# Four edits around a 16-state scan in a fused two-layer kernel: constants loaded in the first stage, the first unit in three banks, an output projection by channels, and a gate placed behind the next scan

## The chip, the core and the metric

The kernel runs on one core of one Trainium2 chip. The metric is the device time of one execution in microseconds. Everything is float32. Engines are named as in the profile: PE (TensorE), DVE (VectorE), ACT (ScalarE), POOL (GpSimd), and SP, whose queue issues the DMAs.

## The reference

An image batch `x` of 4 x 128 channels x 64 x 64 goes through two layers.

Layer 0 normalises `x` by groups, computes a score per 4 x 4 patch with two depthwise convolutions, sorts the 256 patches of each image by score, and runs a selective scan over the 4096 pixels in that order. Its inner width is 256, its state 16. With `xz = x1n @ in_proj_w.T` split into `xm` and `z`:

```
xc = silu(conv1d(xm) + b);  dbc = xc @ x_proj_w.T
dt = softplus(dt_low @ dt_proj_w.T + dt_proj_b)
h  = exp(dt * A) * h + dt * B * xc          # 256 x 16 states, step by step
y  = (h . C + D * xc) * silu(z);  out_m = y @ out_proj_w.T
```

`out_m` is put back into the pixel order and added to `x`. Layer 1 runs a scan with 256 states over the 4096 tokens of each image, adds its output, and then adds a spectral convolution with 16 filters. This second layer takes most of the time and none of its arithmetic is touched here.

## The kernel before

The program is one function, `conv_attn_hybrid` (L1504), with three stages.

**First stage**, `layer0_front` (L24): the four images one after the other, `tokens` (normalising, turning into patches) of the next image beside `ordered` (convolutions, scores, sorting) of this one, plus the matrices of the spectral part. The order of its instructions is written by a planner with costs, not by hand. At its end each image's sorted tokens, `xn`, are evicted from PSUM by eight ACT instructions (L293) and stored to `xnt` in DRAM (L295). The permutation goes to `permd`.

**Scan stage**, `layer0_scan` (L338), whose order is written out by hand (`manual_schedule`). The work is cut into 32 units, 8 per image, of 512 tokens. A unit has 16 steps: two halves of 256 tokens by 8 pairs of states. All 512 steps run in one loop (L632). In step `j` the loop issues: the loads of B and C for `j+5` (`fetch`, SP), the scan's input for `j+3` (`spread`, POOL), the scan's factors for `j+1` (`lift`, four Exp on ACT), the scan itself, its product with C and a copy of the last state (`scan`, DVE), and the sum over states of step `j-1` (`add_up`, two PE matmuls into the bank `y`, and at the end of a half two more with `diag`, which holds D). When a half is complete, `gated` (L581) multiplies `y` by the silu of z on DVE; `y` has one PSUM bank, so the next half's first `add_up` waits for it.

Beside the steps, `beside` (L607) moves three kinds of work forward through one more PSUM bank, `mm`: `project` (the next unit's projections: convolution as four matmuls with premultiplied taps, z, Silu, B/C/dt, Softplus), `output` (out_proj of the finished unit) and `put_back` (permutation back, and the sum with the image). Each is a generator; a step lets at most one of them use `mm` ("mm"), and its eviction ("post") follows a step later.

Before the loop the stage loads its constants through SP (L364 to L380), among them all four permutations (`perm_t`), prepares some on DVE and ACT, and runs `project` of the first unit from start to end, one bank, one step after another (L602). Before that, `layer1_weights` (L750) puts the loads of layer 1's weights on SP. `output` computes, for each of the 16 pixels of a patch, 32 patches x 128 channels, with the gated values as weights of the matmul (L462): 32 rows of the array's output. `put_back` loads half an image into `xs`, which has one buffer, at the moment it needs it (L476).

**Layer 1**, `layer1` (L906): 8192 steps of a 256-state scan (L1314), in an order written by hand.

## Time and profile before

| | us |
|---|---|
| median of three runs | 21104.62 (21103.96 to 21105.43) |
| profiled execution, its own time | 21106.96 |
| its span, first to last instruction | 21105.0 |
| first stage, to the last store of `xnt` (L295) | 0 to 548 |
| scans of the 16-state stage (L554), first to last start | 614.78 to 2674.68 |
| scans of layer 1 (L1314), first to last start | 2710.48 to 20998.3 |
| DVE busy | 20433.2 (97%) |
| POOL busy | 19751.2 (94%) |
| PE busy | 17551.7 (83%) |
| ACT busy | 15761.0 (75%) |

A group of the profile names line, engine, operation, what is written and what is read, shape and count; behind the bar stand busy time and the mean duration of one in ns, then the idle time of the engine just before these instructions and what ended most of it. In the order of time, a row has start, duration, engine, line, operation, count and, in brackets, idle time and its releaser. A matmul of float32 leaves two records.

### The profile page before, as it was taken

The page shows a single profiled execution, that of the slowest core. Times are in us where ns is not written, and L with a number is a line of the kernel's source. Part 1 is how long each engine was busy: PE and PEld are TensorE (multiplying, and loading weights), DVE is VectorE, ACT ScalarE, POOL GpSimd, SP SyncE. Part 2 cuts the span into 40 slices and gives each one's busy share as a digit, 9 for nine tenths or more (in the row PEclk, how much of TensorE's full clock was granted, in tenths as well). Part 3 has the DMA queues.
Part 4 walks back from the last instruction along what each step waited for, and adds up shares of the span by engine and source line. Part 5 has one row for each costly group of instructions (what it writes and reads, how often), then busy time and mean ns, then how long its engine had stood idle before and what let it go on. Part 6 is the DMA issues. An engine that isn't in the chain of part 4 may idle for free.

```text
span 21105.0 us, 282109 instructions
## 1 busy us (share of the span) xinstructions
PE 17551.7 (83%) x99112; PEld 7740.7 (37%) x99112; DVE 20433.2 (97%) x11824; ACT 15761.0 (75%) x28195; POOL 19751.2 (94%) x3541
## 2 busy tenths in 40 slices
PE   7788844655858888877868999599999999999998
PEld 4344421322323333343323344243434434434434
DVE  7799999999999999999999999999999999999997
ACT  3667667777777777777777777787887777788876
POOL 2666699999999999999999999999999999999997
PEclk8999966776979999998979999699999999999999
DMA  1555554555656666665656777577777777777775
GB/s 69 133 142 143 145 162 156 183 174 172 219 174 224 222 226 224 222 211 196 210 186 223 231 239 238 173 238 236 238 235 232 235 234 235 237 235 233 232 231 182
DMA packets 2194842, 4287.94 MB, mean 203 GB/s; under 512 B 768744, under 2 KB 1288208, under 8 KB 1928080
## 3 DMA queue, kind: packets, MB, share of 16 engines
q1 hardware_dynamic: 2193424, 4269.90, 63.3%
q8 instruction: 784, 12.85, 0.2%
q14 instruction: 634, 5.19, 0.1%
HBM read 3645.09 MB, written 623.91 MB: 202 GB/s over the span
## 4 chain that ended last, share of the span: by engine, by line
DVE 51%; issue 15%; PE 12%; POOL 5%; ACT 4%; DMA 1%; DVEq 0%; SPq 0%; POOLq 0%; ACTq 0%
DVE ring L1314 49%; PE conv L1257 6%; POOL ring L1298 4%; PE yp L1344 3%; ACT da L1310 2%; PE fin L1199 1%; ACT conved L1269 1%; DMA strip<-in_phi 0%; ACT t L804 0%; PE mm L883 0%; PE mm L877 0%; PE mm L868 0%; PE mm L1039 0%; PE conv L1111 0%; ACT ye L1351 0%
## 5 line engine op out<-in xcount | busy, mean ns | idle before, releaser
L1298 POOL TENSOR_TENSOR ring<-u,dlb 128x4088 f32<-128x4088 f32 x2048 | 18075.4, 8889 | 67.4 <-DMA dlb<-delta 37.7
L1314 DVE TENSOR_TENSOR_SCAN ring<-da,ring 128x1024 f32<-128x1024 f32 x8192 | 17927.7, 2263 | 180.4 <-ACT da L1310 149.6
L1310 ACT ACTIVATE da<-dlb,at 128x511 f32<-128x511 f32 x16384 | 11321.1, 691 | 4049.2 <-DVE ring L1314 3763.3
L1257 PE MATMUL conv<-strip,tok 128*128 128x512 f32 (+3 forms) x20224 | 8569.6, 551 | 46.0 <-DMA strip<-in_phi 45.0
L1344 PE MATMUL yp<-ring,c 128*32 128x256 f32 x65536 | 4917.1, 428 | 2493.9 <-DVE ring L1314 1283.8
L1257 PEld LDWEIGHTS conv<-strip,tok 128*128 128x128 f32 x20224 | 3606.1, 191 | 4105.8 <-issue 3722.3
L1344 PEld LDWEIGHTS yp<-ring,c 128*32 128x32 f32 x65536 | 2007.5, 119 | 6188.5 <-issue 3468.9
L532 POOL TENSOR_TENSOR v<-dx,bcb 128x1024 f32<-128x1024 f32 x512 | 1208.8, 2361 | 633.0 <-DVE states L554 629.4
L1199 PE MATMUL fin<-conved,pq 128*128 128x512 f32 (+1 forms) x3840 | 1750.5, 549 | 9.2 <-ACT sum L1220 4.8
L546 ACT ACTIVATE f<-dt,an 128x255 f32<-128x255 f32 x2048 | 974.7, 476 | 493.0 <-DVE states L554 442.3
L554 DVE TENSOR_TENSOR_SCAN states<-f,v 128x1024 f32<-128x1024 f32 x512 | 1176.0, 2297 | 106.3 <-ACT f L546 54.7
L1351 ACT COPY ye<-yp 128x512 f32<-128x512 f32 x2048 | 1185.9, 579 | 24.5 <-PE yp L1344 23.4
L570 PE MATMUL y<-p,ident 128*128 128x512 f32 x2048 | 1008.6, 618 | 173.5 <-DVE p L558 170.0
L1269 ACT COPY conved<-conv 128x512 f32<-128x512 f32 x1664 | 963.0, 579 | 146.3 <-PE conv L1257 143.2
L1199 PEld LDWEIGHTS fin<-conved,pq 128*128 128x128 f32 x3840 | 644.5, 192 | 385.8 <-issue 278.0
L558 DVE TENSOR_TENSOR p<-states,bcb 128x1024 f32<-128x1024 f32 x512 | 627.0, 1225 | 38.3 <-DVE states L554 0.5
L570 PEld LDWEIGHTS y<-p,ident 128*128 128x128 f32 x2048 | 363.6, 193 | 709.1 <-issue 336.8
L1304 ACT COPY ring<-vf 128x8 f32<-128x8 f32 x2048 | 386.8, 189 | 4.1 <-DMA omd<-om 4.1
L462 PE MATMUL mm<-ow,yg 128*32 128x128 f32 x2048 | 250.8, 276 | 39.2 <-ACT om L466 37.7
L462 PEld LDWEIGHTS mm<-ow,yg 128*32 128x32 f32 x2048 | 219.3, 133 | 136.4 <-ACT om L466 60.8
L1357 ACT COPY last<-ring 128x8 f32<-128x8 f32 x1792 | 267.2, 198 | 0.0
L407 PE MATMUL mm<-xin,taps 128*128 128x512 f32 x512 | 236.4, 605 | 23.2 <-DVE f L384 20.0
(242 smaller groups left out, 5484.3 us busy)
## 6 DMA issues: line engine op xcount, KB each, us to landing
dlb<-delta SPq DMA_DIRECT2D x2048, 1024.0 KB, 5.3
strip<-in_phi SPq DMA_DIRECT2D x1536, 448.0 KB, 5.0
yd<-ye SPq DMA_DIRECT2D x2048, 256.0 KB, 4.6
bcb<-bcd SPq DMA_DIRECT2D x1024, 256.0 KB, 4.3
strip<-in_phi SPq DMA_DIRECT2D x1024, 256.0 KB, 4.9
pq<-pqd SPq DMA_DIRECT2D x1408, 64.0 KB, 4.4
yt<-yd SPq DMA_DIRECT2D x4096, 4.0 KB, 4.4
pq<-pqd SPq DMA_DIRECT2D x256, 128.0 KB, 4.2
```

The source lines that it names most:

```text
L532: nc.gpsimd.tensor_tensor(v, ready[n][2][:, :, bass.ts(i, SUB)].unsqueeze(1).broadcast_to((128, 2, 2, SUB)), bc[:, 0].unsqueeze(2).broadca ...
L546: nc.scalar.activation(factors[j % 2][:, a, k, 1:], ready[n][1][:, k, SUB * i + 1 : SUB * i + SUB], AF.Exp, scale=an[:, k, 2 * g + a : 2 * ...
L554: nc.vector.tensor_tensor_scan(states.rearrange(flat), factors[j % 2].rearrange(flat), v.rearrange(flat), 0.0, ALU.mult, ALU.add)
L570: nc.tensor.matmul(t.rearrange("p k t -> p (k t)"), ident, p[:, a].rearrange("p k t -> p (k t)"), start=g == 0 and a == 0, stop=False, ski ...
L1199: nc.tensor.matmul(fin[:, bass.ds(c0, w)], pq[:, n, :], u[:, bass.ds(c0, w)], start=begin and n == 0, stop=end and not partly, skip_group_ ...
L1257: nc.tensor.matmul(ps[:, skip:], tok[:, 1 - r if side else r, j, :], strip[:, bass.ds(c0 - lo, TS - skip)], start=which == 0 and j == js[0 ...
L1269: nc.scalar.copy(u[:, cols], ps[:, cols])
L1298: nc.gpsimd.tensor_tensor(ring[:, q % NQ, :, :, 1:], ready[0][:, :, 1:].unsqueeze(1).broadcast_to((128, VD, 2, TS - 1)), dl[:, :, 1:].unsq ...
L1310: nc.scalar.activation(da[:, h, 1:], dl[:, d % VD, 1:], AF.Exp, scale=at[:, h, d : d + 1])
L1314: nc.vector.tensor_tensor_scan(v, da.rearrange("p h t -> p (h t)"), v, 0.0, ALU.mult, ALU.add)
L1344: nc.tensor.matmul(yp[i // 2][bass.ts(p, 32), i % 2], c[:, h, t], moving(h, 128 * i + 32 * p, 32), start=h == 0, stop=h == 1,)
L1351: nc.scalar.copy(ye, yp[j].rearrange("p i d t -> p i t d"))
```

## The change

- `scan_constants` allocates the scan stage's constants before the first stage. `bring` issues their loads in the first stage while its second image is worked on, `prepare` computes with them during the third. `perm_t` is no longer loaded whole.
- In the first stage, four of the last image's eight evictions of `xn` go to DVE.
- The first unit is projected by `opening`, which uses the banks `mm` and `y` and the two of `states`, splits the Silu, takes its last product on DVE and issues the factors of steps 0 and 1. The second unit's projection is begun (its `xin` load) before it.
- `output` first multiplies all 512 tokens by `out_proj_w` with channels as rows, copies that (`yo`), and then turns it with matmuls against the identity: five turns at the bank `mm` and not four.
- `put_back`'s two halves of the image and its permutation are loaded when the output of an image's last unit begins (`place_of`), into two buffers.
- `gated` is issued between the scan and the product of the next step but one, and in that step `beside` goes ahead of `add_up`.
- Layer 1's weights are loaded in step 10 of the scan stage and not before it. The tile `om` gets a pool of its own, and the pools are in another order.

```diff
@@ layer0_front
-            nc.scalar.activation(ranked[:, o : o + 2, :], ps, AF.Identity, bias=nb, scale=ng)
+            if b == NB - 1 and o % 4:
+                nc.vector.tensor_scalar(ranked[:, o : o + 2, :], ps, ng, nb, ALU.mult, ALU.add)
+            else:
+                nc.scalar.activation(ranked[:, o : o + 2, :], ps, AF.Identity, bias=nb, scale=ng)
...
         first.go(1)
+        if b == 1:
+            bring()
+        if b == 2:
+            prepare()
@@ new
+def scan_constants(nc, cp, w, ident):
...
+    def bring():
+        for t, src in to:
+            nc.sync.dma_start(t, src)
+
+    def prepare():
+        for i in range(4):
+            nc.vector.tensor_tensor(taps[:, i, :], taps[:, i, :], win[:, 0:256], ALU.mult)
+        for k in range(2):
+            nc.vector.tensor_scalar(diag[:, k, :], ident, dd[:, k : k + 1], None, ALU.mult)
+        nc.scalar.activation(an, an, AF.Exp)
+        nc.vector.tensor_scalar(an, an, -1.0, None, ALU.mult)
@@ layer0_scan
-    cp = ctx.enter_context(tc.tile_pool(name="b_c", bufs=1))
+    rare = ctx.enter_context(tc.tile_pool(name="b_om", bufs=1))
+    sm = ctx.enter_context(tc.tile_pool(name="b_sm", bufs=1))
     big = ctx.enter_context(tc.tile_pool(name="b_big", bufs=2))
-    sm = ctx.enter_context(tc.tile_pool(name="b_sm", bufs=1))
...
+    def opening(into, xin):
+        xz, dt, dx, af, bcd = into
+        z = states.rearrange("p n k t -> p n (k t)")
+        other = lambda: ps_.tile([128, 512], F32, tag="y", name="other")
+        banks = middle(), other()
+        for k in range(2):
+            for i in range(4):
+                nc.tensor.matmul(
+                    banks[k], taps[:, i, bass.ts(k, 128)], xin[:, bass.ds(i, PJ)], start=i == 0, stop=i == 3
+                )
+            nc.scalar.activation(xz[:, k, :], banks[k], AF.Identity, bias=cb[:, k : k + 1])
+        for k in range(2):
+            nc.tensor.matmul(z[:, k], win[:, bass.ts(2 + k, 128)], xin[:, 3:], start=True, stop=True)
+        nc.vector.tensor_copy(xz[:, 2:4, :], z)
+        nc.scalar.activation(xz[:, 0:2, :], xz[:, 0:2, :], AF.Silu)
+        ps = middle()
+        for k in range(2):
+            nc.tensor.matmul(ps[:96], xw[:, k, :], xz[:, k, :], start=k == 0, stop=k == 1)
+        nc.scalar.activation(xz[:, 2:4, :], xz[:, 2:4, :], AF.Silu)
...
+        banks = other(), middle()
+        for k in range(2):
+            nc.tensor.matmul(banks[k], dw[:, bass.ts(k, 128)], bc[0:8, :], start=True, stop=True)
+            nc.scalar.activation(dt[:, k, :], banks[k], AF.Identity, bias=db[:, k : k + 1])
+        nc.scalar.activation(dt, dt, AF.Softplus)
+        nc.vector.tensor_tensor(dx, dt, xz[:, 0:2, :], ALU.mult)
+        lift(0)
+        lift(1)
+        factors_of_carry(dt, af)
@@ output
-        yr = yg.rearrange("p k (r o) -> p k o r", o=16)
         rows = bass.ts(unit % 4, 32)
+        if unit == L // PJ - 1 and b < NB - 1:
+            for h in range(2):
+                place_of(b, h)
+        yield "mm"
+        ps = middle()
+        for k in range(2):
+            nc.tensor.matmul(ps, ow[:, k, :], yg[:, k, :], start=k == 0, stop=k == 1)
+        yield "post"
+        yo = sm.tile([128, PJ], F32, tag="yo", name="yo")
+        nc.scalar.copy(yo, ps)
+        yr = yo.rearrange("c (r o) -> c o r", o=16)
         for o in range(0, 16, 4):
             yield "mm"
             ps = middle()
             for i in range(4):
-                for k in range(2):
-                    nc.tensor.matmul(
-                        ps[rows, bass.ts(i, 128)], yr[:, k, o + i, :], ow[:, k, :], start=k == 0, stop=k == 1
-                    )
+                nc.tensor.matmul(ps[rows, bass.ts(i, 128)], yr[:, o + i, :], ident, start=True, stop=True)
@@ put_back
+    def place_of(b, h):
+        xs = sm.tile([128, 8, 4, 64], F32, tag="xs", name="xs", bufs=2)
+        nc.sync.dma_start(xs.rearrange("c py oy x -> c (py oy x)"), x[b][:, bass.ts(h, L // 2)])
+        perm = sm.tile([128, 2, 128], F32, tag="perm", name="perm", bufs=2)
+        nc.sync.dma_start(perm, permd[:, b, :, bass.ts(h, 128)])
+        places.append((xs, perm))
@@ scan
         nc.vector.tensor_tensor_scan(
             states.rearrange(flat), factors[j % 2].rearrange(flat), v.rearrange(flat), 0.0, ALU.mult, ALU.add
         )
+        if gate:
+            gated(j - 2)
@@ the loop over steps
-    for _ in project(*units[0], ready[0]):
-        pass
-    fronts, extra, rear, holder = [], [], None, None
-    ahead = [1]
+    xin = big.tile([128, 3 + PJ], F32, tag="xin", name="xin")
+    nc.sync.dma_start(xin, xnt[0][:, 0 : 3 + PJ])
+    ready[1] = tiles()
+    fronts, extra, rear, holder = [Work(project(*units[1], ready[1]))], [], None, None
+    opening(ready[0], xin)
+    ahead = [2]
...
-        if 0 <= j + 1 < steps:
+        if 1 < j + 1 < steps:
             lift(j + 1)
...
-        if j >= 2 and (j - 2) % pairs == pairs - 1:
-            gated(j - 2)
-        prods[j] = scan(j, vs.pop(j), bcs.pop(j))
+        if j == 10:
+            load_weights()
+        gate = j >= 2 and (j - 2) % pairs == pairs - 1
+        prods[j] = scan(j, vs.pop(j), bcs.pop(j), gate)
+        if gate:
+            beside(j)
         if j:
             add_up(j - 1, prods.pop(j - 1))
-        beside(j)
+        if not gate:
+            beside(j)
@@ conv_attn_hybrid
+    early = ExitStack()
+    constants = early.enter_context(tc.tile_pool(name="b_c", bufs=1, side="right"))
+    consts, bring, prepare = scan_constants(nc, constants, w, ident)
+    layer0_front(tc, ident, half, w, x, xnt, permd, pqd, mud, bring, prepare)
...
+    early.close()
     layer1(tc, ident, weights, work, psum, second, w["phi"], pqd, mud, x, omd, permd, first, x2, x3, out)
```

More of the change, by code (lines that the diff above doesn't have):

```diff
@@ L23, in layer0_front @@
 @with_exitstack
-def layer0_front(ctx: ExitStack, tc, ident, half, w, x, xnt, permd, pqd, mud):
+def layer0_front(ctx: ExitStack, tc, ident, half, w, x, xnt, permd, pqd, mud, bring, prepare):
     nc = tc.nc
@@ L334, with later, halves, layer0_scan @@
 PJ = 512
+def scan_constants(nc, cp, w, ident):
+    to = []
+    def later(name, shape, src):
+        t = cp.tile(shape, F32, name=name)
+        to.append((t, src))
+        return t
+    def halves(name, src):
+        return later(name, [128, 2], src.rearrange("(k p) -> p k", p=128))
+    win = later("win", [128, 512], w["in_proj_w"])
+    taps = later("taps", [128, 4, 256], w["conv1d_w"].partition_broadcast(128))
+    cb = halves("cb", w["conv1d_b"])
+    xw = later("xw", [128, 2, 96], w["x_proj_w"].rearrange("(k p) m -> p k m", p=128))
+    dw = later("dw", [8, 256], w["dt_proj_w"])
+    db = halves("db", w["dt_proj_b"])
+    dd = halves("dd", w["D"])
+    an = later("an", [128, 2, NS], w["A_log"].rearrange("(k p) n -> p k n", p=128))
+    ow = later("ow", [128, 2, 128], w["out_proj_w"].rearrange("(k p) c -> p k c", p=128))
+    diag = cp.tile([128, 2, 128], F32, name="diag")
+    last = cp.tile([128, NS, 2], F32, name="last")
+    def bring():
[8 more added lines that the diff above has]
+        nc.vector.tensor_scalar(an, an, -1.0, None, ALU.mult)
+    return (win, taps, cb, xw, dw, db, diag, an, ow, last), bring, prepare
 @with_exitstack
-def layer0_scan(ctx: ExitStack, tc, ident, w, x, xnt, permd, x2, omd, psum, following):
+def layer0_scan(ctx: ExitStack, tc, ident, x, xnt, permd, x2, omd, psum, following, consts, load_weights):
     nc = tc.nc
     ctx.enter_context(tc.manual_schedule())
-    cp = ctx.enter_context(tc.tile_pool(name="b_c", bufs=1))
+    rare = ctx.enter_context(tc.tile_pool(name="b_om", bufs=1))
+    sm = ctx.enter_context(tc.tile_pool(name="b_sm", bufs=1))
     big = ctx.enter_context(tc.tile_pool(name="b_big", bufs=2))
-    sm = ctx.enter_context(tc.tile_pool(name="b_sm", bufs=1))
     wk = ctx.enter_context(tc.tile_pool(name="b_wk", bufs=3))
@@ L354, in layer0_scan @@
     ps_ = ctx.enter_context(tc.tile_pool(name="b_ps", bufs=1, space=PSUM))
-    def load(name, shape, src):
-        t = cp.tile(shape, F32, name=name)
-        nc.sync.dma_start(t, src)
-        return t
-    def halves(name, src):
-        return load(name, [128, 2], src.rearrange("(k p) -> p k", p=128))
-    win = load("win", [128, 512], w["in_proj_w"])
-    perm_t = load("perm_t", [128, NB, 2, 256], permd)
-    taps = load("taps", [128, 4, 256], w["conv1d_w"].partition_broadcast(128))
-    for i in range(4):
-        nc.vector.tensor_tensor(taps[:, i, :], taps[:, i, :], win[:, 0:256], ALU.mult)
-    cb = halves("cb", w["conv1d_b"])
-    xw = load("xw", [128, 2, 96], w["x_proj_w"].rearrange("(k p) m -> p k m", p=128))
-    dw = load("dw", [8, 256], w["dt_proj_w"])
-    db = halves("db", w["dt_proj_b"])
-    dd = halves("dd", w["D"])
-    diag = cp.tile([128, 2, 128], F32, name="diag")
-    for k in range(2):
-        nc.vector.tensor_scalar(diag[:, k, :], ident, dd[:, k : k + 1], None, ALU.mult)
-    an = load("an", [128, 2, NS], w["A_log"].rearrange("(k p) n -> p k n", p=128))
-    nc.scalar.activation(an, an, AF.Exp)
-    nc.vector.tensor_scalar(an, an, -1.0, None, ALU.mult)
-    ow = load("ow", [128, 2, 128], w["out_proj_w"].rearrange("(k p) c -> p k c", p=128))
-    last = cp.tile([128, NS, 2], F32, name="last")
+    win, taps, cb, xw, dw, db, diag, an, ow, last = consts
     factors = [pa.tile([128, 2, 2, SUB], F32, name=f"f{i}") for i in range(2)]
@@ L443, in project, with factors_of_carry @@
         yield "free"
+        factors_of_carry(dt, af)
+    def factors_of_carry(dt, af):
         for i in range(PJ // SUB):
@@ L448, in project @@
                 )
+    def opening(into, xin):
[17 more added lines that the diff above has]
+        nc.scalar.activation(xz[:, 2:4, :], xz[:, 2:4, :], AF.Silu)
+        bc = big.tile([96, PJ], F32, tag="bc", name="bc")
+        nc.scalar.copy(bc, ps[:96])
+        nc.sync.dma_start(bcd[0], bc[32 : 32 + NS, :])
+        nc.sync.dma_start(bcd[1], bc[64 : 64 + NS, :])
+        banks = other(), middle()
[6 more added lines that the diff above has]
+        lift(1)
+        factors_of_carry(dt, af)
@@ L450, in output @@
     def output(b, unit, yg):
         if unit == 0:
-            oms[b] = big.tile([128, 2, 16, 128], F32, tag="om", name="om", bufs=1)
+            oms[b] = rare.tile([128, 2, 16, 128], F32, tag="om", name="om")
         om = oms[b]
-        yr = yg.rearrange("p k (r o) -> p k o r", o=16)
         rows = bass.ts(unit % 4, 32)
+        if unit == L // PJ - 1 and b < NB - 1:
[5 more added lines that the diff above has]
+            nc.tensor.matmul(ps, ow[:, k, :], yg[:, k, :], start=k == 0, stop=k == 1)
@@ L460, in output @@
             for i in range(4):
-                for k in range(2):
-                    nc.tensor.matmul(
-                        ps[rows, bass.ts(i, 128)], yr[:, k, o + i, :], ow[:, k, :], start=k == 0, stop=k == 1
-                    )
+                nc.tensor.matmul(ps[rows, bass.ts(i, 128)], yr[:, o + i, :], ident, start=True, stop=True)
             yield "post"
@@ L468, in output @@
             )
+    places = []
+    def place_of(b, h):
[4 more added lines that the diff above has]
+        places.append((xs, perm))
     def put_back(b):
@@ L473, in put_back @@
         for h in range(2):
-            xs = sm.tile([128, 8, 4, 64], F32, tag="xs", name="xs")
             cols = bass.ts(h, L // 2)
-            nc.sync.dma_start(xs.rearrange("c py oy x -> c (py oy x)"), x[b][:, cols])
+            xs, perm = places.pop(0)
             for oy in range(4):
@@ L482, in put_back @@
                         nc.tensor.matmul(
-                            ps[:, bass.ts(ox, 128)], om[:, r, 4 * oy + ox, :], perm_t[:, b, r, bass.ts(h, 128)],
+                            ps[:, bass.ts(ox, 128)], om[:, r, 4 * oy + ox, :], perm[:, r, :],
                             start=r == 0, stop=r == 1,
@@ L549, in lift, with scan @@
                 )
-    def scan(j, v, bc):
+    def scan(j, v, bc, gate):
         n, i, g = place(j)
@@ L751, in layer1_weights, with load @@
     win = pool.tile([128, 512], F32, name="win")
-    nc.sync.dma_start(win, w_in)
     wbd = pool.tile([128, 2, 512], F32, name="wbd")
-    for t, s in ((wbd[:, :, 0:256], w_b), (wbd[:, :, 256:512], w_delta)):
-        nc.sync.dma_start(t, s.rearrange("(k p) n -> p k n", p=128))
     wo = pool.tile([128, 2, 128], F32, name="wo")
-    nc.sync.dma_start(wo, w_out.rearrange("(k p) n -> p k n", p=128))
     at = pool.tile([128, 2, 256], F32, name="at")
-    nc.sync.dma_start(at, a_t.rearrange("(k p) d -> p k d", p=128))
-    return win, wbd, w_c.rearrange("(k p) n -> p k n", p=128), wo, at
+    def load():
+        nc.sync.dma_start(win, w_in)
+        for t, s in ((wbd[:, :, 0:256], w_b), (wbd[:, :, 256:512], w_delta)):
+            nc.sync.dma_start(t, s.rearrange("(k p) n -> p k n", p=128))
+        nc.sync.dma_start(wo, w_out.rearrange("(k p) n -> p k n", p=128))
+        nc.sync.dma_start(at, a_t.rearrange("(k p) d -> p k d", p=128))
+    return (win, wbd, w_c.rearrange("(k p) n -> p k n", p=128), wo, at), load
 def projection(ctx, tc, ident, half, weights, x2, psum, second):
@@ L1519, in conv_attn_hybrid @@
     omd = dram.tile([2, 128, 16, 128], F32, name="omd")
-    layer0_front(tc, ident, half, w, x, xnt, permd, pqd, mud)
+    early = ExitStack()
+    constants = early.enter_context(tc.tile_pool(name="b_c", bufs=1, side="right"))
+    consts, bring, prepare = scan_constants(nc, constants, w, ident)
+    layer0_front(tc, ident, half, w, x, xnt, permd, pqd, mud, bring, prepare)
     pool = ctx.enter_context(tc.tile_pool(name="weights", bufs=1))
-    weights = layer1_weights(nc, pool, *(w[k] for k in ("W_in", "W_delta", "W_B", "W_C", "W_out", "A")))
+    weights, load_weights = layer1_weights(nc, pool, *(w[k] for k in ("W_in", "W_delta", "W_B", "W_C", "W_out", "A")))
     psum, second = [], []
@@ L1525, in conv_attn_hybrid @@
     first = work[-2](0)
-    layer0_scan(tc, ident, w, x, xnt, permd, x2, omd, psum, work[-1](0, 0, first))
+    layer0_scan(tc, ident, x, xnt, permd, x2, omd, psum, work[-1](0, 0, first), consts, load_weights)
+    early.close()
     layer1(tc, ident, weights, work, psum, second, w["phi"], pqd, mud, x, omd, permd, first, x2, x3, out)
```

## The prediction

> **What bounds the kernel now.** I read the page first, then the waits of the 16-state scan stage, then the order of time at its two ends and at one unit boundary inside it.

> ```profile
> DVE 51%; issue 15%; PE 12%; POOL 5%; ACT 4%; DMA 1%; DVEq 0%; SPq 0%; POOLq 0%; ACTq 0%
> L1314 DVE TENSOR_TENSOR_SCAN ring<-da,ring 128x1024 f32<-128x1024 f32 x8192 | 17927.7, 2263 | 180.4 <-ACT da L1310 149.6
> L554 DVE TENSOR_TENSOR_SCAN states<-f,v 128x1024 f32<-128x1024 f32 x512 | 1176.0, 2297 | 106.3 <-ACT f L546 54.7
> ```

> The 256-state scan of layer 1 (L1314) starts at 2710.5 us and fills the other 18,394 us; no instruction in it is edited. What the change can win lies in the first 2710 us. There the 512 scans of L554 start between 614.8 and 2674.7. An undisturbed step takes 3.81 us from scan to scan: scan 2.30, product L558 1.23, copy L559 0.15 and the gaps. So VectorE sets the pace, and whatever makes it wait in this stage is on the path:

> ```profile
> DVE states L554 <- ACT f L546: 54.7, 33, 48.2
> DVE yg L586 <- PE y L576: 51.9, 37, 2.2
> DVE xs L488 <- DMA xs<-in_x: 23.7, 6, 7.6
> ```

> Columns: total us, times, longest. Three things to win: the 48.2 us before the first scan, the gate's waits, and put_back's image load. At the start of the stage:

> ```profile
> 547.81 0.32 SPq L295 DMA_DIRECT2D xnt<-xn  x1
> 548.18 0.42 SPq L752 DMA_DIRECT2D win<-in_W_in  x1
> 555.78 0.34 SPq L358 DMA_DIRECT2D win<-in_in_proj_w  x1
> 563.32 0.34 SPq L399 DMA_DIRECT2D xin<-xnt  x1
> 566.56 6.09 PE L407 MATMUL mm<-xin,taps 128*128 128x512 f32 x8 [20.02 <-DVE f L384]
> 614.78 2.30 DVE L554 TENSOR_TENSOR_SCAN states<-f,v 128x1024 f32<-128x1024 f32 x1 [48.21 <-ACT f L546]
> ```

> SP sits until 555.78, when the last store of xnt has landed, because the stage's memory lies over that of the first stage; then it loads ten constants and only then xin.

> **Constants in the first stage.** PE started at 566.56. Now SP can issue xin directly behind the store. Ends: a load of 256 KB issued there before (W_in at 548.18) took 8.2 us to land, 556.4; if xin's memory must still wait for the store, 555.78 plus xin's own 2.9 us, 558.7; if it neither queues nor waits, about 551.1. The stage's big pool still lies over the first stage, so I take 558.7: **-7.9** (to -15.5). In exchange the first stage gets the nine loads (4.0 us of SP issue, by their rows), VectorE 1.43 (taps) + 0.48 (diag) + 0.18 (an) = 2.1 us, and ScalarE an Exp of 0.23 plus two table loads of 1.28. SP has slack there; ScalarE is busy 27.3 of the 50 us from 300, VectorE 35.6 and pacing the convolutions, so 0 to 4.9, taken 2.0. The last four of the batch's eight evictions shared with VectorE: PE sets their 1.73 us rhythm, only the last one counts: 1.20 against about 0.69 (L586, also 512 out of PSUM), -0.5. Together **+1.5**.

> **First unit in three banks.** Counted from PE's start; no other work hides this chain. Before, scan 0 came at +48.2, but scan 3 at +60.0 (626.56), since unit 1's projection was already inside. After: convolutions 6.1 + 3.7 without the wait for the eviction, second eviction to +10.5, table load and half a Silu (1.28 + 1.06, as Softplus of 1024) to +12.9, xw 2.0 to +14.9, bc 0.6 to +15.5, two dt's to +18.1, table load and Softplus to +20.5, dx on VectorE 1.2, lift(0) to +23.8, lift(1) +25.8, four af's +26.7. The first scan could start near +25. But unit 1's evictions stand behind all that in ScalarE's queue: convolution 0's at +27.3; convolution 1, on a cold PE again (6.1), +34.4; z's +38.0; table and Silu +41.2; xw (cold, 3.7), bc and dt 0 to +47.4; table and lift(2) +50.7, dt 1, table, Softplus, table, lift(3) to +57.0. So the first scan comes some 23 us earlier and scan 3 only 3: **-3.0** (0 to -12).

> **Gate behind the next scan.** Today's boundary, in order of time:

> ```profile
> 799.38 3.03 PE L424 MATMUL mm<-xz,xw 128*96 128x512 f32 x4 [2.48 <-ACT xz L420]
> 808.62 0.69 DVE L586 TENSOR_TENSOR yg<-y,xz 128x512 f32<-128x512 f32 x1 [2.20 <-PE y L576]
> 809.23 2.29 DVE L554 TENSOR_TENSOR_SCAN states<-f,v 128x1024 f32<-128x1024 f32 x1
> 814.04 2.01 ACT L546 ACTIVATE f<-dt,an 128x255 f32<-128x255 f32 x4
> 816.73 2.30 DVE L554 TENSOR_TENSOR_SCAN states<-f,v 128x1024 f32<-128x1024 f32 x1
> ```

> Of 31 such boundaries 15 wait 2.20 us, 15 wait 0.73, and the gate in mid-unit waits only beside put_back. In the new order the gate is asked 2.3 us later, behind the scan, and y is done: no wait. Queued behind it are the product of the same step, which loses nothing, and on PE the first y matmuls of the next half, because y has one bank; beside's work goes ahead of them, and three p buffers leave two steps. But the next stall is visible: the chain Silu, xw, y, dt, Softplus, table loads, f does not start at the gate. Its f ended at 816.05. Without the wait the scans come at 802.74 + 3.81 = 806.55, then (gate inside: 0.605 issue for the gate, dependent gaps hidden behind it, 4.24) 810.79, and the next wants 814.6. It gets f at 816.1 instead of starting at 816.73. Saved: 0.63 of 2.20. In the short case (scan at 866.62, f to 878.47, scan at 879.15) the same sum gives 870.43, 874.67, 878.52: 0.63 of 0.73. 30 x 0.63 = 18.9; the other 34 gates cost 4.24 against 4.20, +1.4. **-17.5**.

> Why two kinds? The granted clock (column before the DMA share) after the same 2.48 us of idle PE:

> ```profile
> 799.40:802.80 3.40, 3.40 (x5) 0.61 0.77 137
> 863.20:866.60 3.40, 3.33 (x8) 1.00 0.80 152
> ```

> [...] If all turn long, the part is about +3 and the sum -41.

> **Output by channels, then turned.** Per unit before: 4 slots of 16 PE records, 1.96 us each, 7.8 us. After: one slot of 4 records of 512 (1.7) and 4 of 8 records (about 1.0), 5.6 us, plus one ScalarE copy (0.58) and one more slot. Counting slots by the code, a unit's projection and five output slots still fit into 16 steps, put_back finishes one step later, the following layer's projection two steps later and 15 before the end. PE's saving lies beside VectorE's scans: 0. At the end of the stage it is bare: 4 x 2.63 = 10.5 us before, 2.6 + 4 x 1.66 = 9.2 after, **-1.3**.

> **put_back's loads at the start of the last unit's output.** The waits of 23.7 us go, and so do those of the gates next to it (0.60, 1.27, 1.27, 1.52, 1.28, 1.28: 7.2). SP issues 2 MB at once ahead of bcb loads; such a load of 2 MB took 8 us in the first stage, and bcb has two steps (7.6 us) before POOL wants it, POOL another 10 before its scan. 1 us kept for that: **-30** (-20 to -31).

> **Layer 1's weights at step 10.** 4.8 us of SP issue and 1.15 MB, covered by the same lead: 0. Uncovered it would cost some 5 us once.

> **Handover.** The last om has its own pool, so the delta load and ring need no longer wait for the om store (issued about 2692.6, load issued 2696.59): **-3.8** (0 to -5).

> Sum: -7.9 + 1.5 - 3.0 - 17.5 - 30 - 1.3 - 3.8 = **-62**. The profiled execution took 21,106.96 (span 21,105.0 and 2 around it), which gives 21,045; against the median of 21,104.62 the same -62 gives 21,043.

> **Rivals.** [...] (2) *The stall moves entirely to f*: -41, 21,063. ScalarE's order is unchanged, which speaks for it; half of the boundaries being short speaks against. (3) *The image loads crowd out bcb*: two thirds of put_back's gain come back, -42, also 21,063; POOL waited for bcb only twice so far (3.6 us). (4) *Slower: PE stays at half clock through the whole boundary chain*, because it now has less output work and waits for the gate too. Its 16 records of 0.427 and 4 of 0.21 (7.7 us) would take 7.7 more, all of it in front of f: 30 x 7.7 = 231 against the 44 us of waits and some 42 of other gains, +145, 21,250. It eats all gains from 2.9 us a boundary and is slower by 0.2% from 4.3. Against it: in the long kind the clock recovers within 3.4 us (1.47 us lost).

> **How the numbers follow.** 0.2% is about what a measurement of this kernel can tell: 42 us. My case 0.52 (21,025 to 21,060 by its own bounds), rival 1 0.15, rivals 2 and 3 0.25, rival 4 and its like 0.08. The first two are faster, and of 2 and 3 a bit less than half; hence faster 0.78, same 0.15, slower 0.07. The range cuts about a tenth at each end: 21,008 to 21,083.

> **What would show it.** Gate rows without idle time before them; f waits of about 1.5 us at the second scan behind half the boundaries; no wait of xs for the image; PE's first taps matmul near 558; the first scan near 584 but the fourth near 616; layer 1's first scan near 2648. Wrong if the planned first stage ends more than 5 us later, if f waits exceed 3 us a boundary, or if layer 1, from its first scan to the end, isn't 18,394 us long within 10.

## The result, and the profile after

The changed kernel took 21035.42 us, the median of 7 runs (21020.12 to 21045.02). The kernel before, run on the same chip, took 21104.62 (7 runs). The ratio is 0.9967, with a 95% interval of 0.9957 to 0.9977, which is 49 to 91 us faster. The forecast was 21,043, with a range of 21,008 to 21,083. The profiled execution of the changed kernel took 21,031.86 us (span 21,030.2).

The page of the kernel after, its chain and its two scan rows:

```profile
DVE 52%; issue 15%; PE 12%; ACT 4%; POOL 4%; DMA 1%; DVEq 0%; SPq 0%; POOLq 0%; ACTq 0%
L1399 DVE TENSOR_TENSOR_SCAN ring<-da,ring 128x1024 f32<-128x1024 f32 x8192 | 17932.8, 2280 | 169.4 <-ACT da L1395 151.6
L628 DVE TENSOR_TENSOR_SCAN states<-f,v 128x1024 f32<-128x1024 f32 x512 | 1176.5, 2298 | 106.1 <-ACT f L620 47.4
```

The scans cost what they cost before. The idle time ahead of the 16-state scan is the same 106 us too, so this page alone could suggest that nothing happened. The waits of VectorE from 480 to 2600 us tell more (total us, times, longest); these are the first two rows:

```profile
DVE states L628 <- ACT f L620: 47.4, 61, 19.0
DVE xz L489 <- PE states L488: 20.2, 1, 20.2
```

Before, the scan waited 54.7 us for f, of which 48.2 stood in front of the first scan. Now the longest single wait is 19.0 (in front of the third scan, below), and the rest is spread over 60 small ones. The row of xz is new; it is the copy of the first unit's z out of PSUM, before any scan, and the time ahead of it was idle before as well. What is gone are two rows: the gate (`yg`) waits nowhere in this window, after 51.9 us before, and `xs` waits for no image, after 23.7. The start of the stage in order of time (start, duration, engine, line, idle before):

```profile
544.83 0.32 SPq L298 DMA_DIRECT2D xnt<-xn  x1
...
551.39 0.32 SPq L679 DMA_DIRECT2D xin<-xnt  x1
...
554.77 5.30 PE L483 MATMUL mm<-xin,taps 128*128 128x512 f32 x8 [11.17 <-DMA xin<-xnt]
...
578.21 2.30 DVE L628 TENSOR_TENSOR_SCAN states<-f,v 128x1024 f32<-128x1024 f32 x1 [2.60 <-POOL v L606]
...
604.64 2.30 DVE L628 TENSOR_TENSOR_SCAN states<-f,v 128x1024 f32<-128x1024 f32 x1 [19.04 <-ACT f L620]
610.93 2.30 DVE L628 TENSOR_TENSOR_SCAN states<-f,v 128x1024 f32<-128x1024 f32 x1 [2.67 <-ACT f L620]
```

The first scan came at 578 instead of 615, but 19.0 us of that went back into a wait of the third scan. The three rows of scans are steps 0, 2 and 3. The load of xin still waits for the store to land: it was issued 6.6 us behind it, and the store took 6.4 us to land.

Cut at the same events, the two profiled executions compare so (us, with the prediction's terms for each stretch):

| stretch | before | after | change | predicted |
|---|---|---|---|---|
| start to last xnt store | 547.8 | 544.8 | -3.0 | +1.5 |
| store to the first taps matmul | 18.75 | 9.94 | -8.8 | -7.9 |
| taps matmul to scan 3 | 60.00 | 56.16 | -3.8 | -3.0 |
| scan 3 to the last of 512 scans | 2048.1 | 1988.4 | -59.7 | -17.5 - 30 |
| last scan to layer 1's first | 35.80 | 35.24 | -0.6 | -1.3 - 3.8 |
| layer 1 | 18394.5 | 18395.6 | +1.1 | 0 |
| sum | | | -74.8 | -62 |

Most of it is the fourth row, which also holds the largest miss. The last row is small beside what it varies by: in the profiled executions of the nine changed kernels layer 1 took 18388.9 to 18406.3 us, and only one of them has an edit that touches it. Differences between kernels are therefore read from the stretches below, and not from the medians alone. One boundary between units in the kernel after, in order of time:

```profile
905.11 2.67 PE L445 MATMUL mm<-xz,xw 128*96 128x512 f32 x4 [2.48 <-ACT xz L441]
...
912.28 2.30 DVE L628 TENSOR_TENSOR_SCAN states<-f,v 128x1024 f32<-128x1024 f32 x1
913.29 1.03 PE L652 MATMUL y<-xz,diag 128*128 128x256 f32 x4
914.49 0.67 DVE L662 TENSOR_TENSOR yg<-y,xz 128x512 f32<-128x512 f32 x1
...
916.49 2.30 DVE L628 TENSOR_TENSOR_SCAN states<-f,v 128x1024 f32<-128x1024 f32 x1
...
919.77 2.00 ACT L620 ACTIVATE f<-dt,an 128x255 f32<-128x255 f32 x4
...
921.86 2.30 DVE L628 TENSOR_TENSOR_SCAN states<-f,v 128x1024 f32<-128x1024 f32 x1 [1.75 <-ACT f L620]
```

The gate comes behind its scan and has no wait. The step that holds it takes 4.21 us from scan to scan (predicted 4.24). The stall is at the next scan, which waits 1.75 us for f (predicted about 1.5). This is a boundary of the long kind. Only 8 of 30 are of it now; 20 are short, with f waits of 0.28, and two beside put_back are neither. Before, it was 15 and 15.

### The profile page after: what moved, and what is told of

Read it like the earlier page. It is cut to its first block, busy times and chain, and to the rows that moved or that the text cites. A ratio compares the mean times of both kernels' runs of the same rounds, so it can differ in the third digit from the quotient of the medians.

```text
span 21030.2 us, 280370 instructions
## 1 busy us (share of the span) xinstructions
PE 17477.3 (83%) x98216; PEld 7645.0 (36%) x98216; DVE 20429.7 (97%) x11830; ACT 15770.7 (75%) x28221; POOL 19741.8 (94%) x3540
## 4 chain that ended last, share of the span: by engine, by line
DVE 52%; issue 15%; PE 12%; ACT 4%; POOL 4%; DMA 1%; SPq 0%; DVEq 0%; POOLq 0%; ACTq 0%
DVE ring L1399 51%; PE conv L1342 6%; POOL ring L1383 4%; PE yp L1429 3%; ACT da L1395 2%; PE fin L1284 1%; ACT conved L1354 1%; DMA strip<-in_phi 0%; PE mm L968 0%; PE mm L962 0%; PE mm L1124 0%; ACT t L889 0%; PE mm L953 0%; ACT ye L1436 0%; PE conv L1196 0%
## 5 line engine op out<-in xcount | busy, mean ns | idle before, releaser
L1342 PE MATMUL conv<-strip,tok 128*128 128x512 f32 (+3 forms) x20224 | 8567.6, 551 | 47.9 <-DMA strip<-in_phi 47.4
L628 DVE TENSOR_TENSOR_SCAN states<-f,v 128x1024 f32<-128x1024 f32 x512 | 1176.5, 2298 | 106.1 <-ACT f L620 47.4
L634 DVE TENSOR_TENSOR p<-states,bcb 128x1024 f32<-128x1024 f32 x512 | 626.3, 1223 | 36.9 <-PE y L646 0.8
L962 PE MATMUL mm<-t,t 128*128 128x512 f32 x256 | 141.1, 678 | 43.4 <-ACT ye L1436 40.1
```

Of the source, the lines that this page charges most:

```text
L628: nc.vector.tensor_tensor_scan(states.rearrange(flat), factors[j % 2].rearrange(flat), v.rearrange(flat), 0.0, ALU.mult, ALU.add)
L1342: nc.tensor.matmul(ps[:, skip:], tok[:, 1 - r if side else r, j, :], strip[:, bass.ds(c0 - lo, TS - skip)], start=which == 0 and j == js[0 ...
```

## The experiments

Times are medians of 4 to 10 runs. The first four kernels share one chip, on which the kernel before took 21106.22; the last four share another, on which it took 21104.99. "The stretch" is the time from scan 3 to the last of the 512 scans: 1988.4 us in the kernel after, 2048.1 in the kernel before.

**The gate ahead of the scan again**, all else as changed:

```
-        prods[j] = scan(j, vs.pop(j), bcs.pop(j), gate)
         if gate:
-            beside(j)
+            gated(j - 2)
+        prods[j] = scan(j, vs.pop(j), bcs.pop(j), False)
         if j:
             add_up(j - 1, prods.pop(j - 1))
-        if not gate:
-            beside(j)
+        beside(j)
```

> The changed kernel with one part undone: the gate stands ahead of the scan again and the beside work behind add_up. My theory (the gate's wait was only partly won, the rest moved to the f wait): the gate rows wait again, 40 to 50 us in total, the f waits of 0.28 and 1.75 behind the boundaries vanish, the stretch from scan 3 to the last scan grows from 1988.4 to about 2009, the total by about 21. Rival A (the whole 44 us of gate waits were won): the stretch grows by 40 to 45. Rival B (the lighter output on PE is what shortened the boundaries, not the gate's place): it grows by less than 8.

It took 21073.52 us, a ratio of 0.9985 (0.9975 to 0.9994). The stretch was 2025.3 us, 36.9 more than in the kernel after. VectorE's waits:

```profile
DVE yg L662 <- PE y L652: 53.1, 37, 2.3
DVE states L628 <- ACT f L620: 28.5, 32, 19.1
```

The gate waits are back at the size of before, and the f waits fall from 47.4 to 28.5. So it is the placing behind the scan that removes 53 us of gate waits and gives 19 back as f waits. In this kernel 14 boundaries are long; in the kernel after 8 are. The waits in these two rows make 34 of the 36.9; what makes the other 3 is not named by the view of the waits. The placing is worth more than the theory had (21) and a little less than rival A (40 to 45).

**The output projection by pixels again:**

```
-        for k in range(2):
-            nc.tensor.matmul(ps, ow[:, k, :], yg[:, k, :], start=k == 0, stop=k == 1)
...
-                nc.tensor.matmul(ps[rows, bass.ts(i, 128)], yr[:, o + i, :], ident, start=True, stop=True)
+                for k in range(2):
+                    nc.tensor.matmul(
+                        ps[rows, bass.ts(i, 128)], yr[:, k, o + i, :], ow[:, k, :], start=k == 0, stop=k == 1
+                    )
```

> The changed kernel with the output projection as before: per pixel, four slots of 16 records. My theory (PE's saving lies beside the scans): scan 3 to last scan stays at 1988 within 5, the end of the stage takes 1.0 to 1.5 us longer (first gate idle to last om copy), the total 0 to +6. Rival B (PE's lighter output made only 9 of the boundaries long where 15 were): the number of f waits above 1 us rises to 15 or more and the stretch by 8 us or more. Rival C (the fifth slot and the extra copy cost something): the stretch gets shorter by more than 3.

It took 21040.65 us, 0.9968 (0.9956 to 0.998), inside the spread of the kernel after. The stretch was 3.2 us longer, with 11 long boundaries instead of 8 (3 x 1.47 = 4.4), and the end of the stage, from the last gate to the last copy of `om`, 0.8 longer. The output projection by itself moves nothing that can be measured, as the prediction's "lies beside VectorE's scans: 0" said; the -1.3 at the end is -0.8.

**put_back's two loads where they are needed:**

```
-        if unit == L // PJ - 1 and b < NB - 1:
-            for h in range(2):
-                place_of(b, h)
...
         for h in range(2):
+            place_of(b, h)
             xs, perm = places.pop(0)
```

The tile of the image has one buffer here instead of two.

> The changed kernel with put_back's image and permutation loaded when each half is needed, into one buffer, as before. My theory: xs waits for the image return, 20 to 26 us in six waits, and with the gate now behind the scan the waits of the neighbouring gates (7.2) do not all return: scan 3 to last scan grows by 24 to 32 us. Rival (the early loads only moved the time, crowding bcb): it grows by less than 10.

It took 21086.21 us, 0.9991 (0.9982 to 1.0), and the stretch grew by 51 us, more than was expected; 4 x 1.47 = 5.9 of it are long boundaries, 12 here and 8 in the kernel after. The reason for the rest is in VectorE's waits, and in SP's queue in the middle of one put_back:

```profile
DVE xs L560 <- PE mm L554: 45.2, 6, 9.9
```

```profile
1180.58 0.34 SPq L563 DMA_DIRECT2D x<-xs  x1
...
1184.49 0.35 SPq L537 DMA_DIRECT2D xs<-in_x  x1
1184.89 0.43 SPq L539 DMA_DIRECT2D perm<-permd  x1
```

`xs` waits for PE, 45.2 us in six waits, and SP's order says for what PE is likely to wait: the permutation's load (1184.89) stands behind the image's (1184.49), and the image's stands behind the store out of the only buffer (1180.58). The kernel before had its permutation ready. So this kernel isn't the undoing that it was meant to be, and its 51 us can't be put down to the image load alone. The next one takes the two loads apart.

**The image alone where it is needed**, the permutation early as in the kernel after:

```
     def place_of(b, h):
-        xs = sm.tile([128, 8, 4, 64], F32, tag="xs", name="xs", bufs=2)
-        nc.sync.dma_start(xs.rearrange("c py oy x -> c (py oy x)"), x[b][:, bass.ts(h, L // 2)])
...
-            xs, perm = places.pop(0)
+            perm = places.pop(0)
+            xs = sm.tile([128, 8, 4, 64], F32, tag="xs", name="xs")
+            nc.sync.dma_start(xs.rearrange("c py oy x -> c (py oy x)"), x[b][:, cols])
```

> The changed kernel with the two image loads of put_back issued when each half is needed, into one buffer, while the permutations are still loaded at the start of the last unit's output. My theory (what cost 45 us in the run with both late was the permutation too, which stood behind the store of the first half on SP, and which the kernel before held ready): xs waits for the image 20 to 27 us in six waits, scan 3 to last scan 1988 + 22 to 30. Rival (the image alone makes the whole loss): +45 or more.

It took 21057.54 us, 0.9977 (0.9967 to 0.9986). The stretch was 23.8 us longer than in the kernel after:

```profile
DVE xs L562 <- DMA xs<-in_x: 20.6, 6, 5.7
```

This is the row of before again (23.7 us, 6 times). The early image load is worth 23.8, and the gate 36.9 by the first experiment. Together that is 60.7 against 59.7 for the whole stretch, so these two edits account for it.

**PE kept at work over the gap.** Two matmuls whose result is overwritten are added in front of xw, the next unit's projection to B, C and dt, for which PE waits 2.48 us:

```
         ps = middle()
+        for _ in range(2):
+            nc.tensor.matmul(ps, ident, xin[:, 3:], start=True, stop=True)
         for k in range(2):
             nc.tensor.matmul(ps[:96], xw[:, k, :], xz[:, k, :], start=k == 0, stop=k == 1)
```

> The changed kernel plus two extra matmuls of ident with xin (1.7 us of PE, result overwritten by xw) in the 2.48 us in which PE waits for Silu ahead of xw. My theory (the long boundaries are PE at half clock after that gap): the f waits of 1.7 us all become 0.28, PE's xw rows read 1.96 us everywhere, scan 3 to last scan shrinks from 1988.4 to about 1975. [...]

It took 21017.51 us, 0.9959 (0.9945 to 0.9973), and the stretch was 10.4 us shorter than in the kernel after. The long boundaries fell from 8 to 1. In the kernel after, xw at the short boundary before the long one shown above, and PE (length of the window, busy, instructions, granted clock, DMA share, GB/s) in two windows around xw, first at the short boundary and then at the long one, read:

```profile
843.22 1.96 PE L445 MATMUL mm<-xz,xw 128*96 128x512 f32 x4 [2.47 <-ACT xz L441]
841.37:844.78 3.41, 1.56 (x4) 1.00 0.65 133
844.78:848.19 3.41, 3.25 (x8) 1.00 0.35 104
902.81:906.22 3.41, 1.11 (x3) 1.00 0.56 138
906.22:909.63 3.41, 3.41 (x5) 0.50 0.39 116
```

And PE with the two added matmuls (4 records), in order of time:

```profile
896.91 1.88 PE L445 MATMUL mm<-xin,ident 128*128 128x512 f32 x4
899.54 1.96 PE L447 MATMUL mm<-xz,xw 128*96 128x512 f32 x4 [0.76 <-ACT xz L441]
...
909.74 3.27 PE L523 MATMUL mm<-yg,ow 128*128 128x512 f32 x4 [1.41 <-DVE yg L664]
912.80 4.03 PE L648 MATMUL y<-p,ident 128*128 128x512 f32 x8
```

With the gap cut from 2.48 to 0.76 us, xw takes its 1.96 us instead of 2.67. So the gap in front of xw is what lets the clock drop there (0.50 in the last window above), and the drop is what makes a boundary long.

Why one gap of 2.48 us drops it and the next doesn't can be read from the traces. In the traces of the kernels before and after, the times at which the granted clock changed lie on a grid: of its stretches at 1.00 or 0.50, 674 before and 628 after, all but the last of each trace are whole multiples of 3.413 us (3.41333) long, within 0.01 us. In the kernel after it fell, among other times, at 906.22, 1155.39, 1220.25 and 1346.54 us, which lie 73, 19 and 37 such steps apart. The windows above end on this grid. The two kernels have the gap 60 times in the stretch (2.45 to 2.61 us). The clock fell at 24, 15 before and 9 after: exactly those where a time of the grid lay between 0.26 us before xw's start and 1.38 us behind it, as at the long boundary above (1.11), and at none of the others, as at the short one (1.56). In the 3.41 us up to the fall PE had been busy for a share of 0.27 to 0.40; with the gap of 0.76 us that the added matmuls leave it is at least 0.78 at the boundary shown, wherever the grid lies. So in these traces the gap makes a fall possible, and its place on the grid decides. With the added matmuls PE still slows down later in the boundary shown: the output's matmul at 909.74 takes 3.27 us, against 1.98 for the same one in the kernel after (916.14). But that is 10.2 us behind xw, and the boundary stays short, with an f wait of 0.28.

**The second unit's projection from step -3**, so that it doesn't stand among the first unit's on ScalarE:

```
         if j < 0:
-            beside(j)
+            if j >= -3:
+                beside(j)
             continue
```

> The changed kernel with the second unit's projection moved forward only from step -3 on (not -9). My theory (what holds scan 2 and scan 3 back after the opening is the second unit's evictions, Silu and Softplus that stand ahead of lift(2) and lift(3) in ScalarE's queue): the 19.0 and 2.7 us f waits of scans 2 and 3 vanish, scan 3 starts at about 592 instead of 610.9, total about -19. Rival (the second unit is needed early, and being late it makes the boundary at step 16 wait instead): waits of 10 us or more between steps 4 and 20, total within 8 of the changed kernel.

It took 21012.02 us, 0.9957 (0.9942 to 0.9972). Scan 3 came at 590.3 instead of 610.9, 20.7 us earlier, and the stretch stayed at 1989.3. The waits for f:

```profile
DVE states L628 <- ACT f L620: 26.8, 61, 1.7
```

The 19 us in front of the third scan are gone. They were the queue on ScalarE, as the prediction had it ("unit 1's evictions stand behind all that in ScalarE's queue"), and the order was a choice.

**The constants brought and prepared between the two stages**, in memory of their own:

```
-        if b == 1:
-            bring()
-        if b == 2:
-            prepare()
...
+    bring()
+    prepare()
     xin = big.tile([128, 3 + PJ], F32, tag="xin", name="xin")
```

> The changed kernel with the nine constants loaded and prepared at the start of the scan stage, ahead of xin, in the same memory of their own. My theory (the start came earlier because xin no longer stands behind loads that wait for the store of xnt; with memory of their own the constants can be issued at once behind that store): PE's first taps matmul starts 10 to 14 us after the last store is issued (9.9 in the changed kernel), total 0 to +4. Rival (it is the early loading itself that counts): 17 to 19 us after it (18.8 in the kernel before), total +7 to +9. On the first stage: if the preparation costs it something, its end comes 1 us or more earlier than 541.9 to 545.0, where the five kernels with it ended it.

It took 21038.99 us, 0.9968 (0.9956 to 0.998), and decides less than it should have. In order of time:

```profile
15.33 0.45 SPq L366 DMA_DIRECT2D taps<-in_conv1d_w  x1
...
542.41 0.32 SPq L298 DMA_DIRECT2D xnt<-xn  x1
542.54 0.43 DVE L370 TENSOR_TENSOR taps<-taps,win 128x256 f32<-128x256 f32 x1
...
552.79 5.12 PE L479 MATMUL mm<-xin,taps 128*128 128x512 f32 x8 [11.62 <-DMA xin<-xnt]
```

The loads still went out at 15 us, far from the place where they are written; only the preparation moved, and it is hidden by the store: its last instruction ends at 544.46, and xin's load goes out at 549.19. The taps matmul came 10.4 us after the store (9.9 in the kernel after). Whether it was the memory of its own or the early loading that let xin go straight behind the store isn't settled: it needs a kernel whose loads do stay late.

**The late start, the added matmuls and an early flip together.** The third edit makes the reversal matrix `flip` of layer 1 once, at the start of the program, in a pool of its own:

```
-    flip = wp.tile([128, 128], F32, name="flip")
...
+    flip = const.tile([128, 128], F32, name="flip")
+    nc.vector.memset(flip, 0.0)
```

> The changed kernel with three edits together: the second unit from step -3 on, the two extra PE matmuls in the gap ahead of xw, and the matrix flip of layer 1 made in the constants at the program's start instead of in memory that waits for the store of om. By the sum of the parts: scan 3 at about 591 (-19), scan 3 to last scan about 1978 (-10), last scan to first scan of layer 1 about 30.5 instead of 35.2 (-4.7, the load of delta landing 5 us after its issue), total about -34, near 21,001. Rival for the handover (delta's load is as late as flip was): it stays at 34 to 36 us.

It took 20997.21 us (20996.69 to 21000.93), 0.9949 (0.9936 to 0.9961): 38 us below the kernel after, 108 below the kernel before. No boundary between units of this layer was long (the longest wait, 1.7 us, is at the first scan of a unit, step 464, where the kernel after has it too):

```profile
DVE states L630 <- ACT f L622: 13.4, 54, 1.7
```

Scan 3 came at 589.8, the stretch took 1977.8. To see the third edit, first the handover to layer 1 in the kernel after:

```profile
2615.82 0.33 SPq L1369 DMA_DIRECT2D dlb<-delta  x1
2616.32 0.32 SPq L737 DMA_DIRECT2D omd<-om  x1
...
2625.23 0.17 DVE L1024 MEMSET flip<- 128x128 f32 x1 [18.66 <-DMA omd<-om]
2625.47 0.29 POOL L1025 TENSOR_SCALAR_AFFINE_SELECT flip<-flip 128x128 f32<-128x128 f32 x1 [36.39 <-DVE da L1033]
2625.73 26.32 POOL L1383 TENSOR_TENSOR ring<-u,dlb 128x4088 f32<-128x4088 f32 x3
...
2634.56 17.59 DVE L1399 TENSOR_TENSOR_SCAN ring<-da,ring 128x1024 f32<-128x1024 f32 x8 [9.10 <-POOL ring L1383]
```

The delta load goes out 0.5 us ahead of om's store; before, it went out when that store had landed. But `flip` now waits for that store, and the first product of layer 1 stands behind `flip` on POOL. With `flip` made early:

```profile
2584.07 0.33 SPq L1366 DMA_DIRECT2D dlb<-delta  x1
2590.99 26.32 POOL L1380 TENSOR_TENSOR ring<-u,dlb 128x4088 f32<-128x4088 f32 x3 [33.67 <-DMA dlb<-delta]
2599.81 11.06 DVE L1396 TENSOR_TENSOR_SCAN ring<-da,ring 128x1024 f32<-128x1024 f32 x5 [25.00 <-POOL ring L1380]
```

POOL now starts 6.9 us behind the delta load's issue instead of 9.9, and the last scan to layer 1's first takes 32.3 us instead of 35.2.

## Why the prediction was right, and where it was not

**Constants in the first stage.** Right, and at the value chosen: "if xin's memory must still wait for the store" held, and -7.9 measured -8.8. The store landed 1.5 us sooner than before (6.4 us after its issue instead of 7.9), now that no 1.15 MB of layer 1's weights follows it; in the kernel before, the three stores of `xnt` with nothing behind them took 6.4 to 6.7. So 1.5 of the 8.8 fit the move of these weights to step 10, which was booked at 0. The +1.5 in the first stage was -3.0 in the profile, but in the six kernels of the experiments that have the very same first stage it ended anywhere from 541.9 to 546.9: a charge of this size, or the -0.5 of the shared evictions in it, can't be told from that spread. The loads went out at 11 to 23 us, earlier than their place in the loop.

**First unit in three banks.** Right, mechanism and size: -3.0 measured -3.8, with the first scan at 578 (forecast 584) and scan 3 at 611 (616). The experiment with the late start confirms the mechanism.

**Gate behind the next scan.** Here the term was mis-sized; its mechanism held. "0.63 of 2.20" and "0.63 of 0.73" are what came: the three steps around a boundary fell from 13.99 to 13.39 us in the long kind and from 12.52 to 11.92 in the short, 0.60 each. What failed is that the stall would stand "behind half the boundaries": 8 of 30 were long, not 15. Seven boundaries that change kind are 7 x 1.47 = 10.3 us. Together with the waits beside put_back, which were booked at -7.2 under the next step, the sum had 24.7 for the gate, and putting it back cost 36.9: six boundaries change kind there (14 against 8), 8.8 us, and the gates in mid-unit, with those beside put_back, gave 8.6 where 5.8 was booked.

The gap in front of xw is the same 2.48 us in both kernels, and at some boundaries of both the clock drops at it, at 15 of 30 before and 9 of 30 after. But the same gap doesn't mean that the share of long boundaries stays, because the length of a unit moves the gap along the grid of 3.413 us. From one xw to the next it was 62.41 us before, or 63.88 with a long boundary: 18 steps of the grid (61.44) and 0.97 or 2.44 us. One of each makes a whole step, so long and short took turns. In the kernel after it is 61.89 or 63.36: 0.45 or 1.92 us over, so that three short ones and a long one make about a step, and by this estimate one boundary in four is long. With the gate ahead of the scan the units are of 62.41 and 63.88 us again, and 14 of 30 are long. The profile before had the numbers to foresee this, and the prediction didn't ask for them. The truth lay between half of them long, the likeliest case, and none.

**put_back's loads.** Right: no wait for the image is left, and the image part, 22.8 of the 30 (23.7 less 1 kept for bcb), measured 23.8. Rival 3 fell, though not as the text had it: the lead of two steps wasn't always enough for bcb, since POOL's waits for it behind scan 3 came to 11.4 us (3.6 before), 3.7 the longest; but POOL's own lead took them up, and no scan of VectorE's waited for POOL.

**Output by channels, layer 1's weights at step 10.** The output beside the scans is right at nothing within the spread, and its -1.3 at the end was -0.8. Of the weights' move, no cost is to be seen, and the 1.5 us of the store above were left out.

**Handover.** Wrong in the step "so the delta load and ring need no longer wait for the om store (-3.8)". The load no longer does. The ring still does, through the memset of `flip`. So the -0.6 of this stretch leaves nothing for it beside the output's -0.8. With `flip` moved the handover gave 3.0, and the load took 6.6 us to land rather than the 5 that the expectation had.

**The sum.** -62 predicted, -74.8 between the profiled executions, -69 between the medians. By stretches, the start was 6.2 us better than forecast, the scans 12.2 better, the handover 4.5 and layer 1 1.1 worse. That the median came within 8 us of the forecast is in part luck: these misses have opposite signs, and the seven runs themselves lie 25 us apart. One of the prediction's sums is off: with the 1.4 of the other gates in it, the case in which all boundaries turn long comes to -40 and not -41. Rival 2 (the stall moves entirely to f) fell, since 53.1 us of gate waits returned only 19 as f waits. Rival 4 fell too: at the long boundaries the loss stays at 1.47 us.

## What to carry to other kernels

When a wait is removed by moving its instruction back, follow the chain behind it to the next operand that is late: the saving is the difference of the two arrivals (here 0.60 of 0.73 or of 2.20 us), not the wait. Work that was put into idle slots is not free at a stage's start, where nothing hides it; there, holding the second unit back brought 20 us that the early first scan alone had not. A stall that comes and goes with a fixed grid of times can change its share when the period of the loop changes, so compare the period with the grid before counting. Before booking a load as free of a store, look for every tile that is laid into the memory the store reads, since a small memset can inherit the wait (here `flip`, 0.17 us of work behind 18.66 us without any).
